# Graph attention with residual and layer norm on one core: own-column rows from the residual's x, a masked turn, and x loaded earlier

## The chip, the cores and the metric

The kernel runs on one core of one Trainium2 chip. Time is device time in microseconds of one execution, the median of several; the profiled execution has a time of its own and a span, which is the stretch from its first to its last recorded instruction.

## The reference

`x` is 4096 x 512, `adj` 4096 x 4096, W 512 x 2048, all float32. Four heads attend over all columns; `adj` is added to the scores.

```python
ht  = (h @ W).reshape(N, 4, 512).transpose(1, 0, 2)
e   = leaky_relu(src[:, :, None] + dst[:, None, :], 0.01) + adj_mat[None]
att = softmax(e, axis=-1)
h_prime = einsum('hij,hjd->hid', att, ht)          # then the mean over heads
x   = layernorm(x + h_prime.mean(0))
```

The entries of `adj` that aren't zero are uniform between 0.05 and 1e9. They are so far apart that the softmax of a row is 1 at the row's largest entry. So the kernel computes, for each row i with its largest column c: out[i] = layernorm(x[i] + x[c] @ (mean of the four heads' W)). It also tests that the largest entries lead by enough, and has a general path for when they don't; with these inputs that path isn't taken. Entries are more frequent at low columns, and the diagonal is always set: so some rows have a c below 128, and some have c = i.

## The kernel before

**Blocks.** The 4096 rows are 32 blocks of 128. Block 0 is rows 0 to 127; block ib from 1 on has on partition p the row 128 + 31 p + ib - 1. A loop over t from 0 to 31 (L546) does several stages for blocks at different distances: at t it reduces block t, looks up the column of block t - 2, and projects block t - 3.

**Loads.** One queue, SP's, takes adj (2 MiB a block, issued five blocks ahead, `load_adj`), W, x and at the end the output. `hold` keeps all of x in SBUF for the residual; W's rows lie in its blocks 16 to 31 at first. `x_at` (L532) says at which t four more blocks of x are queued, ahead of that t's adj: at t = 3, 7, 11, 15 and 18.

**Finding the column.** DVE reduces the 4096 entries of a row to maxima of segments (16 wide up to block 17, then 32, 64 in the last four; `segment_maxima`, L212), takes the largest and its place (L222, L224). POOL makes from the place a row number (`row`, L226) and gathers that segment (`lead`, L230) from `adj` again. Two blocks later DVE finds the place within the segment (L270), POOL adds both to the column (`col`, L272) and gathers the rows of x with these columns (`y`, L255 or L250). POOL runs in the order written, and so do all engines.

**The table.** In blocks 1 to 27 (`TABLED`) a row with c below 128 isn't gathered: `away` adds 8192 (`SKIP`) to its column, which the gather's bounds check drops. Its projected row comes from a table, x[0:128] @ W, held as three bf16 parts `z`: `low` is the place in the table, `spread` makes from it a 128 x 128 choice matrix `pick` (a matmul `px`, then two ACT operations `off` and `pick`), and three bf16 matmuls (L343) add the table's rows. So that the dropped rows of `y` are zero, ACT clears `y` beforehand (`clear_rows`, L245).

**Projection.** TensorE turns `y` by four transposes (`turned_rows`, L284, into `tp`), ACT copies the turn to `yt` (L286), TensorE adds the residual (L296), the table's rows (L343) and four 128 x 512 products with `w_sum` (L303), all into one PSUM tile. ACT takes the statistics and later writes the normalised rows (`finish`, L391).

**The end.** After the loop the last blocks are projected, some statistics go to DVE (`moments`, `factor`, `normalise`), and the last block is done in two halves (L400, L434, L440). `head_norms` gives the bound of the lead test, in three parts at t = 21, 22 and 23 (L473 to L489).

Of the kernel before, what the change touches and what calls it, by code (L numbers as in the profile page):

```python
# [9 lines left out]
F32 = mybir.dt.float32  # L10
BF16 = mybir.dt.bfloat16
U32 = mybir.dt.uint32
# [12 lines left out]
E_EARLY = 16  # L25
E_LAST = 64
EARLY = 18
LAST = 4
SKIP = 8192
TABLED = range(1, 28)  # L30


@with_exitstack
# [40 lines left out]
def leading_rows(ctx, tc, x, adj, W, a, out, ident, leads, any_bad):  # L74
# [23 lines left out]
    adj_pool = ctx.enter_context(tc.tile_pool(name="adj_pool", bufs=AHEAD + 1))  # L98
    y_pool = ctx.enter_context(tc.tile_pool(name="y_pool", bufs=6))
    lead_pool = ctx.enter_context(tc.tile_pool(name="lead_pool", bufs=1))  # L100
    LEADS = (8, 8, LAST)
    once = ctx.enter_context(tc.tile_pool(name="once", bufs=1))
    small = ctx.enter_context(tc.tile_pool(name="small", bufs=5))
    rows = ctx.enter_context(tc.tile_pool(name="rows", bufs=2))
# [44 lines left out]
    load_x(0, 1)  # L149
    for ib in range(KB // 2 + 1, AHEAD):  # L150
        load_adj(ib)
    load_x(1, Q - 1)

    make_identity(nc, ident)
    first = once.tile([P, NB], U32, name="first")
    for e, lo, hi in spans:
        if lo == 0:
            nc.gpsimd.iota(first[:, 0:1], pattern=[[0, 1]], base=0, channel_multiplier=N // e)
            lo = 1
        nc.gpsimd.iota(  # L160
            first[:, lo:hi], pattern=[[N // e, hi - lo]], base=(P + lo - 1) * N // e,
            channel_multiplier=RB * N // e,
        )
    ones = once.tile([P, P], F32, name="ones")
    nc.gpsimd.memset(ones, 1.0)
    width = once.tile([P, len(spans)], U32, name="width")
# [32 lines left out]
    low_of, pick_of = {}, {}  # L199

    def segment_maxima(ib, lo, hi):

# [14 lines left out]
    def find_segment(ib):  # L217
        if ib == NB - 1:
            nc.vector.max(out=top[:, ib, :], in_=best)
            return  # L220
        seg = seg_of.pop(ib)
        nc.vector.max(out=top[:, ib, :], in_=seg)  # L222
        at = at_of[ib] = small.tile([P, 8], U32, name="at")
        nc.vector.max_index(at, top[:, ib, :], seg)  # L224
        row = small.tile([P, 1], U32, name="row")
        nc.gpsimd.tensor_tensor(row, at[:, 0:1], first[:, ib : ib + 1], op=OP.add)  # L226
# [8 lines left out]
        start = at_of[ib] = small.tile([P, 1], U32, name="start")  # L235
        if ib in TABLED:
            away = small.tile([P, 1], F32, name="away")
            nc.gpsimd.tensor_scalar(away, at[:, 0:1], float(P // e), float(SKIP), op0=OP.is_lt, op1=OP.mult)
            nc.gpsimd.tensor_scalar(start, at[:, 0:1], float(e), away, op0=OP.mult, op1=OP.add)
        else:  # L240
            nc.gpsimd.tensor_tensor(start, at[:, 0:1], width[:, k : k + 1], op=OP.mult)

    def clear_rows(ib):
        y = y_t[ib] = y_pool.tile([P, D], F32, name="y")
        nc.scalar.copy(y, zero.to_broadcast([P, D]))  # L245

    def gather_rows(ib, col):
        if ib not in TABLED:
            y = y_t[ib] = y_pool.tile([P, D], F32, name="y")
            nc.gpsimd.indirect_dma_start(  # L250
                out=y, out_offset=None, in_=x,
                in_offset=bass.IndirectOffsetOnAxis(ap=col[:, :1], axis=0),
            )
            return
        nc.gpsimd.indirect_dma_start(  # L255
            out=y_t[ib], out_offset=None, in_=x,
            in_offset=bass.IndirectOffsetOnAxis(ap=col[:, :1], axis=0),
            bounds_check=N - 1, oob_is_err=False,
        )
        low = low_of[ib] = small.tile([P, 1], BF16, name="low")  # L260
        nc.gpsimd.tensor_scalar(low, col, float(SKIP - 1), float(SKIP - 1), op0=OP.max, op1=OP.subtract)

# [3 lines left out]
    def find_column(ib):  # L266
        if ib < BEHIND:
            find_inner(ib)
        within = small.tile([P, 8], U32, name="within")
        nc.vector.max_index(within, top[:, ib, :], lead_of[ib])  # L270
        col = small.tile([P, 1], U32, name="col")
        nc.gpsimd.tensor_tensor(col, at_of.pop(ib), within[:, 0:1], op=OP.add)  # L272
        gather_rows(ib, col)

    def find_column_in_row(ib):
# [2 lines left out]
        nc.vector.max_index(col, top[:, ib, :], adj_t[ib])  # L278
        gather_rows(ib, col)

    def turned_rows(y):
        tp = psum.tile([P, KB, P], F32, name="tp", bufs=2)
        for kb in range(KB):
            nc.tensor.transpose(tp[:, kb, :], y[:, ds(kb, P, KB)], ident)  # L284
        yt = rows.tile([P, KB, P], F32, name="yt")
        nc.scalar.copy(yt, tp)  # L286
        return yt

    def turn(ib):
        yt_of[ib] = turned_rows(y_t.pop(ib))  # L290

    def residual(ib):
        start = ib not in o_ps
# [35 lines left out]
    def spread(ib):  # L329
        where = psum.tile([P, P], F32, name="px", bufs=1)  # L330
        nc.tensor.matmul(where, low_of.pop(ib).to_broadcast([P, P]), ident_b, start=True, stop=True)  # L331
        off = rows.tile([P, P], F32, name="off")
        nc.scalar.activation(off, where, AF.Square, bias=minus)  # L333
        pick = pick_of[ib] = rows.tile([P, P], BF16, name="pick")
        nc.scalar.activation(pick, off, AF.Relu, bias=1.0, scale=-1.0)  # L335
# [193 lines left out]
    def report(pg):  # L529
        nc.vector.tensor_scalar(any_bad, pg, -1.0, float(N), op0=OP.mult, op1=OP.add)  # L530

    x_at = {lo - 1 - lo // (5 * Q): (lo, Q) for lo in range(Q, BEHIND, Q)}  # L532
    squares = list(range(KB * H))
    squares_at = {t: 2 if t < 7 else 1 for t in range(3, 15)}
    COLUMN, PROJECT, STATS = 2, 3, 4
# [10 lines left out]
    for t in range(NB):  # L546
        if t == NB // 2:
            tc.mark_branch_hint_location("general", engines=HINTED)
        if t in x_at:
            load_x(*x_at[t])  # L550
        if t + AHEAD == NB - 1:
            load_x(LATE, 2)
        load_adj(t + AHEAD)
        middle = PIECES if t in END else 1 if t == NB - 1 else 2
        segment_maxima(t, 0, middle)
        if t >= COLUMN and t not in END and t != COLUMN + 1:
            find_column(t - COLUMN)
# [12 lines left out]
        for lo, hi in FACTORS:  # L570
            if t == lag_of(hi):
                nc.vector.reciprocal(sd[:, lo:hi], sd[:, lo:hi])
                if hi < BEHIND:
                    scales(slice(lo, hi))
        if t < 2:
            mean_of_heads(t)
        elif t == 2:
            mean_of_heads(2)
            mean_of_heads(3)
            fill_table()  # L580
        if t == 0:
            square_sums_of_a()
        if 21 <= t < 24:
            head_norms(t - 21)
        ib = t - PROJECT
        if t == NB - 2:
            finish(BEHIND - 3)
            finish(BEHIND - 2)
        if t == NB - 1:
            row_norm(LATE)  # L590
            row_norm(LATE + 1)
            finish(BEHIND - 1)
            residual(LATE + 1)
        if ib >= 0:
            if ib in TABLED:
                spread(ib)
            turn(ib)
            if ib > BEHIND:
                products(ib - 1, KB - 1, KB)
            if ib < BEHIND:  # L600
                residual(ib)
            if ib in TABLED:
                from_table(ib)
            products(ib, 0, KB if ib < BEHIND else KB - 1)
            if ib == 0:
                split_table()
        for _ in range(squares_at.get(t, 0)):
            square_sum_of_w(squares.pop(0))
        if t >= BEHIND + STATS:
            put_by(t - STATS)  # L610
        elif t >= STATS:
            row_norm(t - STATS)
            parked_stats(t - STATS)
        for lo, hi in FACTORS:
            if t == hi - 1 + STATS:
                root(slice(lo, hi))
        for done in FINISHED.get(t, ()):
            finish(done)
# [253 lines left out]
```

## Time and profile before

| | us |
|---|---|
| median of 3 runs (233.75 to 234.14) | 233.87 |
| the profiled execution | 233.53 |
| its span | 232.0 |
| TensorE busy | 197.6 |
| DVE busy | 189.6 |
| ACT busy | 153.2 |
| POOL busy | 111.5 |
| moved by DMA: 96.04 MB, mean 414 GB/s | |

Engines are named PE (TensorE's matmuls), PEld (its weight loads), DVE, ACT, POOL and SP. In a timeline a row begins with its start and its duration in us; in brackets stands the engine's idle time just before it and what ended it. In the chain of waits a row begins with start and duration of one piece. In a list of groups a row gives the count, then busy us, the mean ns of one, and the idle time before them. A row of windows gives the stretch, its length, the busy time of PE, PEld, DVE, ACT and POOL with the counts, TensorE's granted clock, the DMA share and GB/s.

### The profile page before, as it was taken

The numbers are of one execution on the slowest core, as the hardware profiler recorded it, in microseconds if no ns is written. First come the engines' busy times: TensorE is split into PE (matmuls) and PEld (weight loads), VectorE is DVE, ScalarE is ACT, GpSimd is POOL, SyncE is SP. The second block draws the span as 40 slices with busy tenths as digits, with TensorE's granted clock in tenths as the row PEclk, the third lists the DMA queues.
The fourth block names the chain that finished last, engine by engine and source line by source line (L and its number), as shares of the span: only waits on it lengthen the run. The fifth ranks groups of instructions, "written<-read, shape, count | busy, mean of one in ns | idle before, by whom it ended". The sixth has DMA issues, their size and how long they took to land.

```text
span 232.0 us, 2532 instructions
## 1 busy us (share of the span) xinstructions
PE 197.6 (85%) x604; PEld 95.5 (41%) x614; DVE 189.6 (82%) x296; ACT 153.2 (66%) x378; POOL 111.5 (48%) x254
## 2 busy tenths in 40 slices
PE   0069988779099999997999899999999999999990
PEld 0033443334044444443444345454544444545460
DVE  0448289899879997999699959996999999967882
ACT  3003213588075987797998678878888877958872
POOL 4020414525554556355635665554565665637620
PEclk9999999999859999999999999999999999999997
DMA  6999999999999999999999999999999999999995
GB/s 221 426 435 428 433 421 437 425 431 411 440 429 422 420 437 427 429 421 434 418 433 430 417 435 429 419 430 431 426 432 415 419 425 416 419 416 419 420 374 207
DMA packets 13379, 96.04 MB, mean 414 GB/s; under 512 B 2148, under 2 KB 2596, under 8 KB 7984
## 3 DMA queue, kind: packets, MB, share of 16 engines
q1 hardware_dynamic: 9792, 88.08, 90.0%
q0 software_dynamic: 3552, 7.73, 8.5%
q8 instruction: 6, 0.10, 0.2%
q14 instruction: 13, 0.11, 0.1%
q10 hardware_dynamic: 16, 0.02, 0.0%
HBM read 88.51 MB, written 8.39 MB: 418 GB/s over the span
## 4 chain that ended last, share of the span: by engine, by line
DMA 44%; PE 30%; DVE 19%; ACT 2%; issue 1%; POOL 1%; DVEq 0%; POOLq 0%; ACTq 0%
DMA adj_t<-in_adj_dram 39%; PE o L303 19%; DVE seg L212 15%; DMA y<-in_x_dram,col 4%; PE o L296 3%; PE o L343 3%; PE tp L284 3%; PE o L400 2%; DVE at L224 1%; DVE top L222 1%; DMA a_rows<-in_L_gnn_a_dram 1%; DVE inner L264 1%; POOL lead L230 0%; PE o L396 0%; ACT sq L368 0%
## 5 line engine op out<-in xcount | busy, mean ns | idle before, releaser
L212 DVE TENSOR_REDUCE seg<-adj_t 128x128 f32<-128x2048 f32 (+4 forms) x54 | 138.9, 2589 | 27.4 <-DMA adj_t<-in_adj_dram 27.4
L303 PE MATMUL o<-w_sum,yt 128*128 128x512 f32 x248 | 113.5, 598 | 1.1 <-ACT yt L286 0.8
L303 PEld LDWEIGHTS o<-w_sum,yt 128*128 128x128 f32 x248 | 46.8, 192 | 49.0 <-issue 42.0
L230 POOL DMA_INDIRECT lead<-in_adj_dram,row x31 | 32.5, 1050 | 14.5 <-POOL row L226 14.5
L255 POOL DMA_INDIRECT y<-in_x_dram,col x27 | 29.1, 1077 | 12.1 <-POOL col L272 6.1
L226 POOL TENSOR_TENSOR row<-at,first 128x1 uint32<-128x1 uint32 x31 | 5.8, 188 | 60.0 <-DVE at L224 43.6
L284 PE MATMUL tp<-ident,y 128*128 128x128 f32 x128 | 22.9, 302 | 12.0 <-DMA y<-in_x_dram,col 11.9
L286 ACT COPY yt<-tp 128x512 f32<-128x512 f32 x33 | 19.0, 576 | 14.2 <-PE tp L284 13.9
L451 PE MATMUL o<-hold,ident 128*128 128x512 f32 x32 | 16.4, 671 | 14.0 <-DMA hold<-in_L_gnn_W_dram 14.0
L284 PEld LDWEIGHTS tp<-ident,y 128*128 128x128 f32 x128 | 18.3, 210 | 23.9 <-issue 17.8
L296 PE MATMUL o<-hold,ident 128*128 128x512 f32 x50 | 26.5, 612 | 0.0
L333 ACT ACTIVATE off<-px,minus 128x128 f32<-128x128 f32 x27 | 9.9, 366 | 19.9 <-PE px L331 19.8
L343 PE MATMUL o<-z,pick 128*128 128x512 bf16 x72 | 20.4, 386 | 1.1 <-ACT pick L335 0.8
L347 ACT ACTIVATE sq<-hold 128x512 f32<-128x512 f32 x32 | 20.0, 625 | 0.0
L391 ACT ACTIVATE hold<-hold,nm,sd 128x512 f32<-128x512 f32 x24 | 18.8, 801 | 0.0
L374 ACT ACTIVATE sq<-hold,nm 128x512 f32<-128x512 f32 x24 | 17.3, 722 | 0.8
L452 ACT ACTIVATE w_sum<-o 128x512 f32<-128x512 f32 x4 | 2.4, 597 | 22.5 <-PE o L451 22.5
L245 ACT COPY y<-zero 128x512 f32<-128x512 f32 x27 | 16.3, 603 | 0.0
L451 PEld LDWEIGHTS o<-hold,ident 128*128 128x128 f32 x32 | 6.7, 216 | 22.9 <-issue 21.6
L343 PEld LDWEIGHTS <-pick 128*128 128x128 bf16 x81 | 7.8, 100 | 19.9 <-issue 10.5
L372 ACT ACTIVATE hold<-o 128x512 f32<-128x512 f32 x24 | 14.3, 597 | 0.8
L222 DVE MAX8 top<-seg 128x8 f32<-128x256 f32 (+2 forms) x31 | 11.3, 366 | 1.1
(117 smaller groups left out, 190.3 us busy)
## 6 DMA issues: line engine op xcount, KB each, us to landing
adj_t<-in_adj_dram SPq DMA_DIRECT2D x28, 2048.0 KB, 33.1
adj_t<-in_adj_dram SPq DMA_DIRECT2D x6, 1024.0 KB, 27.3
out_dram<-hold SPq DMA_DIRECT2D x12, 512.0 KB, 10.1
hold<-in_x_dram SPq DMA_DIRECT2D x5, 1024.0 KB, 33.0
hold<-in_L_gnn_W_dram SPq DMA_DIRECT2D x2, 2048.0 KB, 16.5
hold<-in_x_dram SPq DMA_DIRECT2D x4, 512.0 KB, 12.7
adj_t<-in_adj_dram SPq DMA_DIRECT2D x4, 512.0 KB, 18.6
out_dram<-hold SPq DMA_DIRECT2D x4, 256.0 KB, 2.8
```

The source lines that it names most:

```text
L212: nc.vector.tensor_reduce(seg_of[ib][:, ts(k, N // e // n)], adj_t[ib][:, ts(k, N // n)].rearrange("p (s e) -> p s e", e=e), axis=AX.X, op ...
L230: nc.gpsimd.indirect_dma_start(out=lead, out_offset=None, in_=adj_segs[e], in_offset=bass.IndirectOffsetOnAxis(ap=row[:, :1], axis=0),)
L255: nc.gpsimd.indirect_dma_start(out=y_t[ib], out_offset=None, in_=x, in_offset=bass.IndirectOffsetOnAxis(ap=col[:, :1], axis=0), bounds_che ...
L284: nc.tensor.transpose(tp[:, kb, :], y[:, ds(kb, P, KB)], ident)
L286: nc.scalar.copy(yt, tp)
L296: nc.tensor.matmul(o_ps[ib], ident, hold[:, ib, :], start=start, stop=False)
L303: nc.tensor.matmul(o_ps[ib], yt_of[ib][:, kb, :], w_sum[:, kb, :], start=(start and kb == 0), stop=(kb == KB - 1),)
L343: nc.tensor.matmul(o_ps[ib], pick, z[k], start=(start and k == 0), stop=False)
L347: nc.scalar.activation(sq, hold[:, ib, :], AF.Square, accum_out=xx[:, ib : ib + 1])
L374: nc.scalar.activation(sq, hold[:, ib, :], AF.Square, bias=nm[:, i], scale=-float(D), accum_out=sd[:, i])
L391: nc.scalar.activation(hold[:, ib, :], o, AF.Identity, bias=nm[:, i], scale=sd[:, i])
L451: nc.tensor.matmul(o, ident, hold[:, w_at + kb * H + h, :], start=(h == 0), stop=(h == H - 1))
```

## The change

- `OWNED` is blocks 4 to 17. There a row whose column is its own row number isn't gathered: POOL compares the column with `own`, a constant, and adds 8192 where they agree (`skipped`, `asked`). Its row of x is in `y` beforehand, since ACT copies the residual's x to `y` in place of zero.
- So `y` holds x also in the rows that come from the table. The turn leaves these out: POOL makes `kept`, a diagonal matrix with 1 where the row's column is below 8192, and TensorE multiplies by it in ordinary f32 matmuls in place of the transposes.
- x must be there sooner: the first load takes blocks 1 to 7, blocks 8, 12 and 16 follow at t = 2, 6 and 10, and block 20 stays at t = 18.
- Blocks 18 and 19 are no longer in the table: all their rows are gathered, and `clear_rows`, `low`, `spread` and the three table matmuls fall away.
- Segments are 64 wide from block 24 on (before from 28).
- `head_norms` runs at t = 16, 17 and 18. `off` is bf16 with one buffer, and there are fewer buffers for `lead`. At the end two finishes stand ahead of a block's moments.

```diff
@@
-LAST = 4
+LAST = 8
 SKIP = 8192
-TABLED = range(1, 28)
+TABLED = (*range(1, 18), *range(20, 28))
+OWNED = range(4, 18)
...
-    LEADS = (8, 8, LAST)
+    LEADS = (4, 4, LAST - 1)
...
-    load_x(1, Q - 1)
+    load_x(1, 2 * Q - 1)
...
+    own = once.tile([P, len(OWNED)], F32, name="own")
+    nc.gpsimd.iota(
+        own, pattern=[[1, len(OWNED)]], base=P + OWNED[0] - 1, channel_multiplier=RB,
+        allow_small_or_imprecise_dtypes=True,
+    )
...
     def clear_rows(ib):
         y = y_t[ib] = y_pool.tile([P, D], F32, name="y")
-        nc.scalar.copy(y, zero.to_broadcast([P, D]))
+        nc.scalar.copy(y, hold[:, ib, :] if ib in OWNED else zero.to_broadcast([P, D]))
+
+    def leave_out_own(ib, col):
+        skipped = small.tile([P, 1], F32, name="skipped", bufs=2)
+        k = ib - OWNED[0]
+        nc.gpsimd.tensor_scalar(skipped, col, own[:, k : k + 1], float(SKIP), op0=OP.is_equal, op1=OP.mult)
+        asked = small.tile([P, 1], U32, name="asked", bufs=2)
+        nc.gpsimd.tensor_scalar(asked, col, skipped, None, op0=OP.add)
+        return asked
+
+    def keep_gathered(ib, col):
+        kept = kept_of[ib] = rows.tile([P, P], F32, name="kept")
+        nc.gpsimd.tensor_scalar(kept, ident, float(SKIP), col, op0=OP.mult, op1=OP.is_gt)
...
+        asked = leave_out_own(ib, col) if ib in OWNED else col
         nc.gpsimd.indirect_dma_start(
             out=y_t[ib], out_offset=None, in_=x,
-            in_offset=bass.IndirectOffsetOnAxis(ap=col[:, :1], axis=0),
+            in_offset=bass.IndirectOffsetOnAxis(ap=asked[:, :1], axis=0),
             bounds_check=N - 1, oob_is_err=False,
         )
+        if ib in OWNED:
+            keep_gathered(ib, col)
...
-            nc.tensor.transpose(tp[:, kb, :], y[:, ds(kb, P, KB)], ident)
+            if kept is None:
+                nc.tensor.transpose(tp[:, kb, :], y[:, ds(kb, P, KB)], ident)
+            else:
+                nc.tensor.matmul(tp[:, kb, :], y[:, ds(kb, P, KB)], kept, start=True, stop=True)
...
-        off = rows.tile([P, P], F32, name="off")
+        off = rows.tile([P, P], BF16, name="off", bufs=1)
...
-    x_at = {lo - 1 - lo // (5 * Q): (lo, Q) for lo in range(Q, BEHIND, Q)}
+    x_at = {2: (8, 4), 6: (12, 4), 10: (16, 4), 18: (20, 4)}
...
-        if 21 <= t < 24:
-            head_norms(t - 21)
+        if 16 <= t < 19:
+            head_norms(t - 16)
...
+    finish(BEHIND + 2)
+    finish(LATE - 1)
     moments(NB - 2)
-    finish(BEHIND + 2)
     stats_of_half(NB - 1, 0)
     factor(NB - 2)
     normalise(NB - 2, o_ps.pop(NB - 2))
-    finish(LATE - 1)
```

On SP the x loads (128x2048) move ahead. Before, from the load of x's blocks 8 to 11 to that of blocks 16 to 19, with block 12's adj the first and block 19's the last between them (the numbers after adj_t only tell tiles apart):

```order
L135 DMA hold_68<-in_x_dram 128x2048
L128 DMA adj_t_492<-in_adj_dram 128x4096
L128 DMA adj_t_550<-in_adj_dram 128x4096
L128 DMA adj_t_607<-in_adj_dram 128x4096
L128 DMA adj_t_664<-in_adj_dram 128x4096
L135 DMA hold_68<-in_x_dram 128x2048
L128 DMA adj_t_725<-in_adj_dram 128x4096
L128 DMA adj_t_784<-in_adj_dram 128x4096
L128 DMA adj_t_841<-in_adj_dram 128x4096
L128 DMA adj_t_898<-in_adj_dram 128x4096
L135 DMA hold_68<-in_x_dram 128x2048
```

Now, from block 14's adj to the load of x's blocks 20 to 23, which stands before block 23's adj as it did:

```order
L129 DMA adj_t_627<-in_adj_dram 128x4096
L136 DMA hold_68<-in_x_dram 128x2048
L129 DMA adj_t_691<-in_adj_dram 128x4096
L129 DMA adj_t_757<-in_adj_dram 128x4096
L129 DMA adj_t_822<-in_adj_dram 128x4096
L129 DMA adj_t_885<-in_adj_dram 128x4096
L129 DMA adj_t_948<-in_adj_dram 128x4096
L129 DMA adj_t_1014<-in_adj_dram 128x4096
L129 DMA adj_t_1080<-in_adj_dram 128x4096
L129 DMA adj_t_1146<-in_adj_dram 128x4096
L136 DMA hold_68<-in_x_dram 128x2048
```

The load of x's blocks 16 to 19 stood ahead of block 20's adj and stands ahead of block 15's now; eight blocks of adj follow it without x between them.

On POOL, one pass of the loop in the middle, from the row number of block t to the place in the table of block t - 2, before:

```order
L226 TENSOR_TENSOR row<-at,first 128x1
L230 DMA lead_617<-in_adj_dram,row 128x16
L238 TENSOR_SCALAR away<-at 128x1
L239 TENSOR_SCALAR start<-at,away 128x1
L272 TENSOR_TENSOR col<-start,within 128x1
L255 DMA y<-in_x_dram,col 128x512
L261 TENSOR_SCALAR low<-col 128x1
```

and now:

```order
L232 TENSOR_TENSOR row<-at,first 128x1
L236 DMA lead_701<-in_adj_dram,row 128x16
L245 TENSOR_SCALAR away<-at 128x1
L246 TENSOR_SCALAR start_f<-at,away 128x1
L297 TENSOR_SCALAR col_f<-within,start_f 128x1
L258 TENSOR_SCALAR skipped<-col_f,own 128x1
L260 TENSOR_SCALAR asked<-col_f,skipped 128x1
L276 DMA y<-in_x_dram,asked 128x512
L265 TENSOR_SCALAR kept<-ident,col_f 128x128
L284 TENSOR_SCALAR low<-col_f 128x1
```

Two operations stand between the column and its gather, and one between the gather and `low`.

On TensorE, the end of block 17 and blocks 18 and 19, now:

```order
L315 MATMUL tp<-kept,y 128x128 x4
L327 MATMUL o<-hold,ident 128x512
L374 LDWEIGHTS pick
L374 MATMUL o<-z_151,pick 128x512
L374 LDWEIGHTS pick
L374 MATMUL o<-z_152,pick 128x512
L374 LDWEIGHTS pick
L374 MATMUL o<-z_153,pick 128x512
L334 MATMUL o<-w_sum,yt 128x512 x4
L313 MATMUL tp<-ident,y 128x128 x4
L327 MATMUL o<-hold,ident 128x512
L334 MATMUL o<-w_sum,yt 128x512 x4
```

Block 17 is turned by `kept`; blocks 18 and 19 are turned by transposes and have no table rows, so that the last three rows stand twice (one of them is shown). Before, each of these blocks had the rows of block 17, with transposes by `ident` in place of `kept`.

More of the change, by code (lines that the diff above doesn't have):

```diff
@@ L198, in leading_rows @@
     seg_of, at_of, lead_of, y_t, yt_of, o_ps = {}, {}, {}, {}, {}, {}
-    low_of, pick_of = {}, {}
+    low_of, pick_of, kept_of = {}, {}, {}
     def segment_maxima(ib, lo, hi):
@@ L234, in find_segment @@
         lead_of[ib] = lead
-        start = at_of[ib] = small.tile([P, 1], U32, name="start")
+        owned = ib in OWNED
+        start = at_of[ib] = small.tile([P, 1], F32 if owned else U32, name="start_f" if owned else "start")
         if ib in TABLED:
@@ L270, in find_column @@
         nc.vector.max_index(within, top[:, ib, :], lead_of[ib])
-        col = small.tile([P, 1], U32, name="col")
-        nc.gpsimd.tensor_tensor(col, at_of.pop(ib), within[:, 0:1], op=OP.add)
+        start = at_of.pop(ib)
+        if ib in OWNED:
+            col = small.tile([P, 1], F32, name="col_f", bufs=2)
+            nc.gpsimd.tensor_scalar(col, within[:, 0:1], start, None, op0=OP.add)
+        else:
+            col = small.tile([P, 1], U32, name="col")
+            nc.gpsimd.tensor_tensor(col, start, within[:, 0:1], op=OP.add)
         gather_rows(ib, col)
@@ L279, in find_column_in_row, with turned_rows @@
         gather_rows(ib, col)
-    def turned_rows(y):
+    def turned_rows(y, kept=None):
         tp = psum.tile([P, KB, P], F32, name="tp", bufs=2)
         for kb in range(KB):
-            nc.tensor.transpose(tp[:, kb, :], y[:, ds(kb, P, KB)], ident)
+            if kept is None:
+                nc.tensor.transpose(tp[:, kb, :], y[:, ds(kb, P, KB)], ident)
+            else:
+                nc.tensor.matmul(tp[:, kb, :], y[:, ds(kb, P, KB)], kept, start=True, stop=True)
         yt = rows.tile([P, KB, P], F32, name="yt")
@@ L289, in turn @@
     def turn(ib):
-        yt_of[ib] = turned_rows(y_t.pop(ib))
+        yt_of[ib] = turned_rows(y_t.pop(ib), kept_of.pop(ib, None))
     def residual(ib):
```

## The prediction

> **What bounds the kernel now.** I read the page's head and slices first, then the chain of waits from its end, then the windows and waits of the stretch that the chain names.
>
> ```profile
> span 232.0 us, 2532 instructions
> DMA  6999999999999999999999999999999999999995
> ```
>
> The DMA engines are busy in every slice but the first and the last, so a first reading says: bytes bound it. The chain says something else about the last third:
>
> ```profile
> 139.45 9.32 DMA y<-in_x_dram,col
> ...
> 148.91 0.72 PE tp L284 x4
> ...
> 150.49 0.65 PE o L343 x3
> 151.13 3.43 PE o L303 x8
> 154.57 0.13 PE o L475 x2
> 154.70 0.31 PE o L476 x2
> ...
> 155.17 0.53 PE tp L284 x4
> ...
> 160.65 0.06 PE px L331
> 160.70 0.54 PE tp L284 x4
> ...
> 166.24 0.54 PE tp L284 x4
> ...
> 222.91 3.73 PE o L400 x16
> ```
>
> The turn (tp) at 148.91 is block 17's, released by that block's gather; 155.17, 160.70 and 166.24 are blocks 18, 19 and 20. From there the chain is TensorE, 5.53 us a block. Its idle time in the window from 149 to 221 us:
>
> ```profile
> 149.00:221.00 72.00, 71.35 (x234) 35.37 (x238) 64.08 (x116) 57.43 (x143) 41.22 (x85) 1.00 1.02 423
> PE tp L284 <- DMA y<-in_x_dram,col: 0.4, 1, 0.4
> ```
>
> TensorE is busy 71.35 of 72 us at clock 1.00 (first PE column), and so is the DMA (share 1.02, 423 GB/s). Its one wait for a gather in there is block 17's. So whatever makes that turn start later, and is not taken out of TensorE's work behind it, ends the program later. Before block 17, from block 4's turn at 71.7 on, TensorE still waits for gathers:
>
> ```profile
> PE tp L284 <- DMA y<-in_x_dram,col: 3.7, 6, 1.3
> ```
>
> **x sooner.** DVE's reductions show when a block of adj is there (blocks 12, 15, 16, 17, 18, 19, 20 and 23, in this order):
>
> ```profile
> 90.17 4.42 DVE L212 TENSOR_REDUCE seg<-adj_t 128x256 f32<-128x4096 f32 x1 [1.42 <-DMA adj_t<-in_adj_dram]
> 107.06 4.39 DVE L212 TENSOR_REDUCE seg<-adj_t 128x256 f32<-128x4096 f32 x1
> 114.50 4.42 DVE L212 TENSOR_REDUCE seg<-adj_t 128x256 f32<-128x4096 f32 x1 [1.77 <-DMA adj_t<-in_adj_dram]
> 120.12 4.42 DVE L212 TENSOR_REDUCE seg<-adj_t 128x256 f32<-128x4096 f32 x1
> 125.74 4.40 DVE L212 TENSOR_REDUCE seg<-adj_t 128x128 f32<-128x4096 f32 x1
> 131.15 4.40 DVE L212 TENSOR_REDUCE seg<-adj_t 128x128 f32<-128x4096 f32 x1
> 139.07 2.29 DVE L212 TENSOR_REDUCE seg<-adj_t 128x64 f32<-128x2048 f32 x1 [2.51 <-DMA adj_t<-in_adj_dram]
> 158.53 2.29 DVE L212 TENSOR_REDUCE seg<-adj_t 128x64 f32<-128x2048 f32 x1 [2.00 <-DMA adj_t<-in_adj_dram]
> ```
>
> Four blocks of x are 1 MiB, at 423 GB/s 2.48 us of the one queue. Before, the waits at 16, 20 and 23 are these loads. In the changed order adj of blocks 16 to 19 stands behind one x load more than before, and adj 15 behind two; from 20 on the count is as it was. Between 90.17 and 114.50 lie four adj blocks and one x load: (24.33 - 2.48) / 4 = 5.46 us a block, so adj 15 landed near 106.6. Two loads more make 111.5; less the rows that are not gathered any more by then (105 of the 145 below, 0.5 us) 111.0. DVE then needs its own pace, 5.62 us a block with segments of 16 and 5.41 with 32, and the head norms' operations, which move from blocks 21 to 23 to blocks 16 to 18; of five groups the first and the last:
>
> ```profile
> L473 DVE TENSOR_SCALAR each<-ident,aa 8x8 f32<-8x8 f32 x1 | 0.2, 199 | 0.0
> L489 DVE TENSOR_REDUCE vn<-both 128x1 f32<-128x4 f32 x1 | 0.2, 157 | 0.0
> ```
>
> 0.85 us in all. Block 19 starts at 111.0 + 5.62 x 3 + 5.41 + 0.85 = 134.1 in place of 131.15: **+2.95 us**. Block 23, with no extra load ahead, keeps its landing or gains the saved bytes.
>
> **POOL.** One pass of POOL, block 19's, with the gather of block 17 in it, and the one row for a 128x128 operation:
>
> ```profile
> 136.43 0.19 POOL L226 TENSOR_TENSOR row<-at,first 128x1 uint32<-128x1 uint32 x1 [0.40 <-DVE inner L264]
> ...
> 138.25 0.25 POOL L238 TENSOR_SCALAR away<-at 128x1 f32<-128x1 uint32 x1
> 138.60 0.27 POOL L239 TENSOR_SCALAR start<-at,away 128x1 uint32<-128x1 uint32 x1
> ...
> 139.45 1.08 POOL L255 DMA_INDIRECT y<-in_x_dram,col  x1 [0.44 <-POOL col L272]
> 140.61 0.23 POOL L261 TENSOR_SCALAR low<-col 128x1 bf16<-128x1 uint32 x1
> 3.01 0.57 POOL L182 TENSOR_SCALAR minus_b<-ident 128x128 bf16<-128x128 f32 x1
> ```
>
> `skipped` and `asked` come ahead of the gather, at 0.35 us from start to start each (138.25 to 138.60): +0.7. `kept` stands behind it, +0.67 by L182's row with the gap; it waits for the turn two blocks back, and `low`, the next `row` and the next gather are queued behind it. A pass grows from 4.4 to 5.8 us, more than DVE's 5.62, so POOL also falls behind, by 0.2 a pass plus the 0.6 of the scales; blocks 18 and 19, out of the table, give back 0.35 each. Between nothing and 1 us of backlog I take 0.5. The gather of block 13 belongs to block 15's pass: 111.0 + 5.3 to that pass's `row` as in block 19 (136.43 less 131.15) + 0.3 for segments of 16, then 3.0 (136.43 to 139.45) + 0.7 to the gather: 120.3. Landing takes:
>
> ```profile
> DMA to landing us min/median/max: 6.1/8.4/9.3
> ```
>
> so 128.7. The gather of block 17: 139.45 + 2.95 + 0.7 + 0.5 - 0.35 = 143.25, landed 151.7.
>
> **The masked turn.** Four transposes take 0.53 us, 0.134 each. An ordinary f32 matmul is two instructions here: 512 columns 0.43 each (L303, 3.43 / 8), 256 columns 0.233 (L400, 3.73 / 16), 16 columns 0.065 (L475). For 128 columns that gives 0.107 (a quarter of L303) up to the transposes' own 0.134: eight of them 0.86 to 1.07. The added cost is 0.33 to 0.54 a block, I take 0.45, nearest to two instructions in place of one at this size. Nothing is the lower bound, should the pair overlap wholly; two instructions in place of one of the same kind can't be a gain. Blocks 4 to 17 gain 14 x 0.45 = 6.3 us of TensorE work against the 3.7 of waits: even with every gather in time TensorE would be late.
>
> The Trainium skill ("TensorE: Matmul & The Clock Gate", Terms) has transpose mode as four times faster for FP32. By that the masked turn would be 2.13 us, +1.6 a block; the trace's 512-column rows put the factor at 1.6 to 2, and I go by them.
>
> **Sum.** TensorE from block 13's turn: 128.7 + 4 x 5.98 = 152.6 for block 17, a little after its gather, in place of 148.91. Block 18: + 5.98 = 158.6 (155.17 before, with the 0.44 of L475 and L476, which move ahead). Blocks 18 and 19 lose L343 and px, 0.71 each: 163.4 and 168.2 for blocks 19 and 20, against 160.70 and 166.24. So TensorE is 2.0 us late at block 20, with a slack of 0.26 at the last block's gather:
>
> ```profile
> 221.28 0.72 PE L284 MATMUL tp<-ident,y 128*128 128x128 f32 x4 [0.26 <-DMA y<-in_x_dram,col]
> ```
>
> That leaves **+1.7 us**.
>
> Edits at nothing: the copy of x in place of zero is the same 128x512 on ACT; its first one, block 4's, waits for the x load behind adj 4, and the turn's copy of block 0 waits behind it on ACT. What hides that is TensorE's longest wait, ahead of block 3's turn:
>
> ```profile
> 63.42 1.10 PE L284 MATMUL tp<-ident,y 128*128 128x128 f32 x4 [5.76 <-DMA y<-in_x_dram,col]
> ```
>
> Without that cover it would cost up to the 2.5 us of the load. The saved gathers: counting the reference's inputs, 145 rows of blocks 4 to 17 have their own column as maximum, and 47 rows of blocks 18 and 19 are now fetched that came from the table; 98 rows net.
>
> ```profile
> q0 software_dynamic: 3552, 7.73, 8.5%
> ```
>
> 8.5% of 16 x 232 engine-us over 3552 packets is 89 ns; 98 x 89 / 16 = 0.5 us of DMA, which ends no wait of TensorE. Segments of 64:
>
> ```profile
> L222 DVE MAX8 top<-seg 128x8 f32<-128x128 f32 x10 | 3.0, 295 | 0.3
> L224 DVE FIND_INDEX8 at<-top,seg 128x8 uint32<-128x128 f32 x10 | 2.8, 285 | 0.0
> L222 DVE MAX8 top<-seg 128x8 f32<-128x64 f32 x3 | 0.7, 228 | 0.1
> L224 DVE FIND_INDEX8 at<-top,seg 128x8 uint32<-128x64 f32 x3 | 0.7, 220 | 0.0
> ```
>
> 0.13 us a block, 0.5 over four, on a DVE whose gathers then land ahead of a TensorE that is late. The finishes that move ahead of a square root let a pair of blocks be stored sooner; the last store is block 31's, behind L400 at 222.91, and keeps its place.
>
> The profiled execution took 233.53 us, 0.34 under the median 233.87. 233.53 + 1.7 = 235.2 for such an execution, **235.6** as a median.
>
> **Rivals.**
> *Faster: the bytes show.* If gathers land sooner by more than their rows, or the turn is as cheap as the transposes and POOL's additions hide, TensorE reaches block 20 early and the end moves with DVE and DMA: 0.5 of bytes, 0.25 of head norms out of block 23, up to 0.5 from the segments; adj's landing holds it to some 0.6. It decides once block 17's turn starts before 150.6 us (+ 5.98 + 2 x 4.82 = 166.2). For it: the DMA row of nines. Against: 2.95 us of delay stands ahead of that gather. 233.2.
> *No change.* A masked turn of 0.53 and no POOL backlog or addition: gather at 142.4, turn 150.8, block 20 at 150.8 + 5.53 + 2 x 4.82 = 166.0. It is the lower bound of both prices at once. 233.8.
> *POOL waits for TensorE.* `kept` has two buffers. Once a turn starts more than about 3.6 us after its gather landed (two blocks of 5.98 less 8.4 of landing), POOL stands, and the next `row`, gather and so DVE and the adj queue behind it, and every later block repeats it: 235.6 + 3 for three blocks of 1 us, 238.6. By my sum TensorE is 0.9 behind at block 17; it needs a turn of 0.53 + 0.45 + (3.6 - 0.9) / 4 = 1.65 us.
> *Long masked turns.* If an instruction of 128 columns were held as long as one of 256 (0.233, L400), the turn would take 8 x 0.233 = 1.86, +1.33 a block: 14 x 1.33 = 18.6, less 3.7 of waits and 1.4 of the table, 247. L475's 0.065 for 16 columns speaks against so high a floor. The Trainium skill's four times, on the same page, would make some 251.
>
> **How the numbers follow.** Forecast 0.57; faster 0.18; no change 0.14; POOL waits 0.08; long masked turns 0.03. The forecast's own range comes from 0.33 with a landing 0.5 us under the median to 0.54 with one of 9.3: 234.5 to 237.0. To leave no more than 2 in 10 out it reaches from 233.2 (most of the faster case) to 237.8. A measurement of this kernel tells 0.2% (0.47 us) from no change: faster 0.18, same 0.14, slower 0.57 + 0.08 + 0.03 = 0.68.
>
> **What would show it.** In the changed profile: DVE's reduction of block 19 near 134 us, that of block 23 near 158; the gather of block 17 issued at 143 and its turn near 152.6; tp groups of 0.86 to 1.07 us in blocks 4 to 17; TensorE again without waits from there to the last block. Wrong would make it: a turn of block 17 before 150.6 us, waits of TensorE for gathers behind block 20 (then DVE or DMA bounds the end), or tp groups at 0.53.

## The result: 249.5 us, and the profile after

The changed kernel takes 249.52 us (median of 4 runs, 248.75 to 249.75) beside 234.0 us for the kernel before. The ratio is 1.0659 with a 95% interval of 1.0633 to 1.0685: 15.5 us slower, where 1.7 us was forecast. The direction was right, the size was not; the time lies beside the rival that had been given a chance of 0.03.

The page of the changed kernel, first the head and the slices of TensorE and DMA, then the group of the masked turns (`kept`), and from the list of groups that of the plain ones (`ident`):

```profile
span 248.1 us, 2669 instructions
...
PE   0079980689899999999999999999999999999990
...
DMA  6999999999999999999999999999999999955053
...
L315 PE MATMUL tp<-kept,y 128*128 128x128 f32 x112 | 29.2, 404 | 1.3 <-DMA y<-in_x_dram,asked 1.3
```

```profile
L313 PE MATMUL tp<-ident,y 128*128 128x128 f32 x72 | 12.4, 294 | 0.9 <-DMA y<-in_x_dram,col 0.9
```

The DMA engines now run dry before the end (5, 5, 0, 5, 3 in the last five slices), where before they were busy to the last one; TensorE stays busy up to the last slice. The fourteen masked turns (112 instructions) cover 29.2 us, 2.09 each with the overlap into what follows; a plain one (72 instructions, 18 turns, 12.4 us) covers 0.69 by the same count.

The chain of waits of the same kernel (start, length, what) shows what a block now costs on TensorE. Blocks 9, 10, 17, 18, 19 and 20:

```profile
109.05 1.92 PE tp L315 x8
110.97 0.86 PE o L327 x2
111.83 0.65 PE o L374 x3
112.48 3.43 PE o L334 x8
115.91 0.06 PE px L362
115.97 1.92 PE tp L315 x8
...
164.90 1.92 PE tp L315 x8
...
171.76 0.47 PE tp L313 x4
...
176.60 0.47 PE tp L313 x4
...
181.51 0.53 PE tp L313 x4
```

A block lasts 115.97 - 109.05 = 6.92 us in place of 5.53, and the whole difference is the turn: 1.92 in place of 0.53, 0.24 us for each of the eight instructions. Block 17's turn starts at 164.90 (148.91 before, 152.6 forecast), block 20's at 181.51 (166.24 before): + 15.3, and that is carried to the end. The stretches that these rows come from:

```profile
100.00:149.00 49.00, 49.00 (x159) 29.11 (x158) 37.35 (x58) 34.78 (x89) 34.49 (x75) 1.00 1.01 427
149.00:200.00 51.00, 51.00 (x164) 26.86 (x163) 45.20 (x69) 38.36 (x94) 31.43 (x72) 1.00 1.01 423
```

TensorE (the first column behind the length) is busy without a gap from 100 us on, at clock 1.00: the masked turns have made it the bound 50 us sooner than in the kernel before.

The weight loads suggest where the 0.24 us of an instruction of 128 columns come from. First those of the changed kernel's masked turn, then those of a plain turn in the kernel before:

```profile
108.83 1.94 PEld L315 LDWEIGHTS tp<-kept,y 128*128 128x128 f32 x8 [0.33 <-issue]
```

```profile
148.88 0.56 PEld L284 LDWEIGHTS tp<-ident,y 128*128 128x128 f32 x4 [0.92 <-PE px L331]
```

Eight loads back to back fill 1.94 us, 0.24 each, with no idle time between them: the matmuls and their loads go in step. Four loads for the transposes fill 0.56. Which of the two sets the pace, and what makes it so long, none of the forecast's rows showed, and the experiments had to find it.

### The profile page after: what moved, and what is told of

The parts are those of the page before. It is cut to its first block, busy times and chain, and to the rows that moved or that the text cites. A ratio compares the mean times of both kernels' runs of the same rounds, so it can differ in the third digit from the quotient of the medians.

```text
span 248.1 us, 2669 instructions
## 1 busy us (share of the span) xinstructions
PE 213.9 (86%) x662; PEld 113.7 (46%) x662; DVE 189.5 (76%) x296; ACT 151.6 (61%) x372; POOL 131.3 (53%) x293
## 2 busy tenths in 40 slices
DMA packets 13235, 95.90 MB, mean 387 GB/s; under 512 B 2155, under 2 KB 2539, under 8 KB 7840
## 4 chain that ended last, share of the span: by engine, by line
PE 61%; DMA 20%; issue 6%; POOL 4%; DVE 4%; ACT 2%; SPq 0%; POOLq 0%
PE o L334 34%; DMA adj_t<-in_adj_dram 13%; PE tp L315 9%; PE o L327 7%; PE o L374 6%; DMA y<-in_x_dram,col 4%; DMA y<-in_x_dram,asked 3%; PE tp L313 3%; DVE seg L218 2%; POOL lead L236 2%; PE o L431 2%; POOL y L276 1%; PE px L362 1%; POOL away L245 0%; DVE inner L287 0%
## 5 line engine op out<-in xcount | busy, mean ns | idle before, releaser
L315 PE MATMUL tp<-kept,y 128*128 128x128 f32 x112 | 29.2, 404 | 1.3 <-DMA y<-in_x_dram,asked 1.3
L315 PEld LDWEIGHTS tp<-kept,y 128*128 128x128 f32 x112 | 27.2, 326 | 6.1 <-issue 3.3
L482 PE MATMUL o<-hold,ident 128*128 128x512 f32 x32 | 16.3, 669 | 14.3 <-DMA hold<-in_L_gnn_W_dram 14.3
L327 PE MATMUL o<-hold,ident 128*128 128x512 f32 x50 | 25.6, 593 | 0.0
L364 ACT ACTIVATE off<-px,minus 128x128 bf16<-128x128 f32 x25 | 9.1, 366 | 16.9 <-PE px L362 16.8
L276 POOL DMA_INDIRECT y<-in_x_dram,asked x14 | 15.2, 1088 | 6.9 <-POOL asked L260 5.4
L374 PEld LDWEIGHTS <-pick 128*128 128x128 bf16 x75 | 7.2, 98 | 18.9 <-issue 11.1
L276 POOL DMA_INDIRECT y<-in_x_dram,col x11 | 11.9, 1081 | 6.3 <-POOL col L300 3.3
L313 PEld LDWEIGHTS tp<-ident,y 128*128 128x128 f32 x72 | 10.5, 208 | 6.9 <-issue 5.1
(128 smaller groups left out, 249.5 us busy)
```

What stands on the lines that cost most here:

```text
L276: nc.gpsimd.indirect_dma_start(out=y_t[ib], out_offset=None, in_=x, in_offset=bass.IndirectOffsetOnAxis(ap=asked[:, :1], axis=0), bounds_c ...
L315: nc.tensor.matmul(tp[:, kb, :], y[:, ds(kb, P, KB)], kept, start=True, stop=True)
L327: nc.tensor.matmul(o_ps[ib], ident, hold[:, ib, :], start=start, stop=False)
L374: nc.tensor.matmul(o_ps[ib], pick, z[k], start=(start and k == 0), stop=False)
L482: nc.tensor.matmul(o, ident, hold[:, w_at + kb * H + h, :], start=(h == 0), stop=(h == H - 1))
```

## The experiments

Theory A, formed on these rows: the masked turn is the mis-sized term and explains all of the 13.8 us between forecast and result. Theory B: the additions on POOL, or x sooner, cost several us as well, and the long turns hide them. All ratios are against the kernel before, run beside them on the same chip (medians 234.04 to 234.06).

### The turn alone, and everything but the turn

**Ordinary matmuls in the kernel before.** The edit, for blocks 4 to 17 alone:

```
-            nc.tensor.transpose(tp[:, kb, :], y[:, ds(kb, P, KB)], ident)
+            nc.tensor.matmul(tp[:, kb, :], y[:, ds(kb, P, KB)], ident, start=True, stop=True)
```

> The kernel before, with only the turn of blocks 4 to 17 changed from four transposes to four ordinary f32 matmuls with the identity; nothing on POOL, no other edit; the same numbers are computed. Theory A: + 14 x 1.39 = 19.5 us of TensorE, less the 4.1 us that it waited for gathers from block 4 to 17: + 15.4, about 249.2. Rival B (part of the 15.5 us comes from POOL, x or the table): 238 to 246. The prediction's own price (+0.45 a block): 236.

Measured: 247.75 us, ratio 1.0593 (1.0577 to 1.0609), + 13.7. Turns of 1.92 us from block 4's at 71.74 to block 17's at 161.61: 89.87 / 13 = 6.91 a block, so 5.53 + 1.39 as in the changed kernel. TensorE's own waits in that stretch took up 5.3 us (71.72 to 148.91 is 77.2 for 13 blocks of 5.53), a little more than the 4.1 expected. The exchange of transposes for ordinary matmuls, with nothing else changed, is worth nearly all of the result. Theory A holds this far.

**The changed kernel with transposes**, POOL's masks still made:

```
-                nc.tensor.matmul(tp[:, kb, :], y[:, ds(kb, P, KB)], kept, start=True, stop=True)
+                nc.tensor.transpose(tp[:, kb, :], y[:, ds(kb, P, KB)], ident)
```

> The changed kernel with the turn of blocks 4 to 17 back to four transposes; POOL still makes the masks, x is still sooner, 18 and 19 still out of the table. The mask is left out, so rows of these blocks that the table serves get their own row of x added. Theory A (the masked turn alone is the mis-sized term: 1.92 us in the changed trace in place of 0.53): tp groups of 0.53, the rest as the prediction's sum without its masked term: block 17's turn about 151.7, block 20 near 166.9, time 233.8 to 234.8. Rival B (the additions on POOL or the earlier x cost several us as well, hidden behind the long turns): 236 or more, with waits of TensorE for gathers behind block 17.

Measured: 241.34 us, ratio 1.0303 (1.0282 to 1.0323), + 7.3. Theory A expected at most 234.8. So a second cost of some 7 us stood behind the first, and theory B has a part in it. POOL's timeline in that run, from block 16's `row` to block 17's, with the gather of block 14 between them (start, length, idle time before and what ended it):

```profile
126.88 0.19 POOL L232 TENSOR_TENSOR row<-at,first 128x1 uint32<-128x1 uint32 x1
127.35 1.07 POOL L236 DMA_INDIRECT lead<-in_adj_dram,row  x1 [0.28 <-POOL row L232]
128.50 0.24 POOL L245 TENSOR_SCALAR away<-at 128x1 f32<-128x1 uint32 x1
128.85 0.27 POOL L246 TENSOR_SCALAR start_f<-at,away 128x1 f32<-128x1 uint32 x1
129.23 0.29 POOL L297 TENSOR_SCALAR col_f<-within,start_f 128x1 f32<-128x1 uint32 x1
129.62 0.31 POOL L258 TENSOR_SCALAR skipped<-col_f,own 128x1 f32<-128x1 f32 x1
130.02 0.29 POOL L260 TENSOR_SCALAR asked<-col_f,skipped 128x1 uint32<-128x1 f32 x1
130.83 1.08 POOL L276 DMA_INDIRECT y<-in_x_dram,asked  x1 [0.51 <-POOL asked L260]
131.97 0.75 POOL L265 TENSOR_SCALAR kept<-ident,col_f 128x128 f32<-128x128 f32 x1
132.81 0.23 POOL L284 TENSOR_SCALAR low<-col_f 128x1 bf16<-128x1 f32 x1
133.13 0.19 POOL L232 TENSOR_TENSOR row<-at,first 128x1 uint32<-128x1 uint32 x1
```

From `row` to `row` are 6.25 us, and nothing in it waits for another engine: the gaps of 0.28 and 0.51 are POOL's own, ahead of a gather. POOL's gathers go at this pace from block 6's at 79.71 to block 12's at 117.82 (38.11 / 6 = 6.35, with the two small operations for the scales that follow some passes), and block 17's is issued at 148.89, where 143.25 was forecast and 139.45 stood before. From 75.75 to 145.51 no `row` waits for DVE any more, so nothing takes the lateness up in between. The busy time would not have told it: 61.3 us of the 83 between 66 and 149, some three quarters.

**The same without `kept` on POOL** (with transposes nothing reads it):

```
-        if ib in OWNED:
-            keep_gathered(ib, col)
```

> The run with the turn by transposes, and without the 128x128 mask on POOL (which nothing reads there). The mask is left out, so rows that the table serves get their own row of x added. Theory P (in that run POOL is what bounds blocks 5 to 17: a pass of 6.25 us without a wait, row to row, so each pass adds to the lateness): pass 6.25 - 0.84 = 5.41, under DVE's 5.62, POOL waits for DVE again, the gather of block 17 goes from 148.9 to 143 to 145, time 241.3 to 234.5 to 236. Theory H (DVE is held: the head norms, moved to blocks 16 to 18, make DVE wait for their products on TensorE, which stand behind a late turn, 4.6 us in that run): the gather of block 17 stays past 146, time 237.5 or more. Theory X (x sooner is what costs): time stays at 239 or more.

Measured: 236.55 us, ratio 1.0099 (1.0064 to 1.0135), + 2.5. One operation off POOL gives 4.8 us back; block 17's gather is issued at 143.66, as theory P had it. POOL's pass is the second cost, shown by the removal of its longest addition. Theory H (DVE waits for the head norms' products on TensorE) is not what held this run: that wait shrinks from 4.6 to 0.9 us by itself. So part of the 4.8 may have come by way of it, set off by POOL's late gathers; how much was not separated. The time is a little above P's range, too.

**x sooner alone**, in the kernel before:

```
-    load_x(1, Q - 1)
+    load_x(1, 2 * Q - 1)
...
-    x_at = {lo - 1 - lo // (5 * Q): (lo, Q) for lo in range(Q, BEHIND, Q)}
+    x_at = {2: (8, 4), 6: (12, 4), 10: (16, 4), 18: (20, 4)}
```

> The kernel before with only the loads of x in the changed order: seven blocks ahead of block 5's adj, then 8, 12 and 16 ahead of adj 7, 11 and 15. The prediction's step: DVE's reduction of block 19 at 131.15 + 2.95 - 0.85 (no head norms) = 133.3, block 23 unchanged; gather of block 17 at 141.6, its turn about 150.0, block 20 near 167.4, + 1.1: 235.0. Rival: the delay is taken up by waits that are there anyway: 233.5 to 234.4. Theory X (x sooner alone costs several us): 236 or more.

Measured: 235.88 us, ratio 1.0076 (1.006 to 1.0093), + 1.8. DVE's reduction of block 15 starts at 111.42 (adj 15 was forecast there at 111.0 to 111.5), of block 19 at 133.69 (133.3 expected), of block 23 at 158.59 (158.53 before). Its chain:

```profile
150.66 0.72 PE tp L284 x4
156.92 0.53 PE tp L284 x4
162.45 0.53 PE tp L284 x4
167.98 0.53 PE tp L284 x4
```

Block 17's turn at 150.66 (150.0 expected), block 20's at 167.98 (167.4), 1.74 behind the 166.24 of before. The landings were read rightly; the price at the end is 0.7 us above the expected one, and it is as much alone as the whole forecast.

### What makes the masked turn's loads long

Three theories stood for the 0.24 us of an instruction with 128 columns: its weight load (W), the columns streamed (C, and L for load and stream one after the other), and the step of four elements with which the load goes through y (S). In the kernels with 64 columns four transposes fill the tile first, and half of it stays unmasked. In those without a step, or with a step of two, products go with other rows of W than they should.

```
 as changed      nc.tensor.matmul(tp[:, kb, :], y[:, ds(kb, P, KB)], kept, ...)
 64 columns      nc.tensor.matmul(tp[:, kb, : P // 2], y[:, ds(kb, P, KB)], kept[:, : P // 2], ...)
 no step         nc.tensor.matmul(tp[:, kb, :], y[:, ts(kb, P)], kept, ...)
 step of two     nc.tensor.matmul(tp[:, kb, :], y[:, ds(kb // 2 * 2 * P + kb % 2, P, 2)], kept, ...)
 no step, 64     nc.tensor.matmul(tp[:, kb, : P // 2], y[:, ts(kb, P)], kept[:, : P // 2], ...)
```

> The changed kernel; ahead of the eight instructions of each masked turn stand four transposes that fill the tile, and the eight stream 64 columns of the mask in place of 128 (the other half of the tile is left unmasked). Theory W (each instruction lasts as long as the load of its own 128 columns of weights, 0.24 us, however few columns are streamed): tp groups 0.47 + 1.92 = 2.4 us, time 249.5 + 11 x 0.47 = 254 to 256. Theory C (time goes with the columns streamed, 0.24 for 128, so 0.12 for 64): 0.47 + 0.96 = 1.43, time about 243 to 245. Theory L (load and stream one after the other, 0.13 + 0.107): 0.47 + 1.49 = 1.96, time about 250.

> The changed kernel, with the turn of blocks 4 to 17 taking its weights from 128 neighbouring columns of y in place of every fourth one (so these blocks' products go with other rows of W than they should). Theory W: no change, tp groups 1.92, time 249.5. Theory S (the step of four elements makes the load of weights slow; loads of neighbouring columns are shown with 0.19): groups of 1.55 or less, time 245.5 or less.

> The changed kernel with the masked turn's weights taken from every second column of y (so products go with other rows of W). Runs so far: a step of four 0.24 us an instruction, neighbouring columns 0.119. Theory B (the load's time goes with the bytes that it passes over, four times as many with a step of four): 0.12 to 0.13, tp groups 0.95 to 1.05, time about 240. Theory A (any step makes the load slow): 0.24, groups 1.92, time 249.5.

> The changed kernel with the masked turn's weights from neighbouring columns and only 64 columns of the mask streamed, behind four transposes that fill the tile (as in the run with 64 columns and the step of four, where the eight instructions took 1.80 us). Theory 1 (neighbouring columns: the 128 streamed columns set the 0.119): the eight take 0.43 to 0.55, tp groups with the transposes about 1.0. Theory 2 (the load itself takes about 0.11 also without a step): the eight take 0.85 to 0.95, groups 1.35 to 1.45.

One row of each run's chain, in this order: the eight masked instructions in steady work.

```profile
97.76 1.80 PE tp L318 x8
```

```profile
150.32 0.95 PE tp L315 x8
```

```profile
152.13 1.00 PE tp L315 x8
```

```profile
115.26 0.84 PE tp L318 x8
```

| step | columns streamed | eight instructions | each |
|---|---|---|---|
| 4 | 128 | 1.92 us | 0.24 us |
| 4 | 64 | 1.80 us | 0.225 us |
| 2 | 128 | 1.00 us | 0.125 us |
| 1 | 128 | 0.95 us | 0.119 us |
| 1 | 64 | 0.84 us | 0.105 us |

Half the columns save 0.015 us an instruction: C and L fall. The step of four doubles it, a step of two hardly costs anything, so W holds in the form of S: the instruction goes at the pace of its weight load, some 0.105 us for 128 neighbouring f32 columns, and 0.225 to 0.24 with 16 bytes from one column to the next. (The 0.105 is no floor of every instruction: L475's two in the forecast's rows, the first of which had been loaded under a longer instruction, took 0.065 each.) Theory S had expected 1.55, from a 0.19 that is the length of a single load, not its pace; theory B of the step of two is right in the figure, but by its reason (the bytes passed over) a load of neighbours would take 0.06, and the last run shows 0.105, as its theory 2 had it (0.84 for the eight, 0.85 to 0.95 expected).

This price of the step is shown for ordinary f32 matmuls alone. The transposes load the same columns with the same step, and their four loads fill 0.56 us, 0.14 each. Why the step of four doubles the one and not the other, no run here settles.

The Trainium skill ("TensorE: Matmul & The Clock Gate", LDWEIGHTS) gives a load as its columns divided by 1.2 in ns. For 128 that is an estimate of 107 ns, and the 0.105 of the last run agrees. The formula counts columns and nothing else; at a step of four the measured 0.24 decides.

The times: 257.18, 240.05, 242.23 and 244.58 us, one run each. With the step gone the turn is 0.95 and the kernel is still 6.0 us slower than before: TensorE then waits for gathers again (4.3 us in seven waits), and POOL issues these some 6.2 us apart, as in the run with transposes. In the run with 64 columns and step four, `kept` waited 9.1 us for TensorE, the forecast's third rival; in the changed kernel itself it was 1.7 us in two waits.

### Three mends, and the small edits alone

**The changed kernel, whole, with three mends:** weights from neighbouring columns with W loaded to match, `kept` made on DVE behind the next block's reduction, and the head norms at blocks 21 to 23 again. The turn's edit is the line "no step" above; two more:

```
-    w_blocks = W.rearrange("(p kb) (h d) -> p (kb h) d", p=P, h=H)
+    w_blocks = W.rearrange("(kb p) (h d) -> p kb h d", p=P, h=H)
...
-        nc.gpsimd.tensor_scalar(kept, ident, float(SKIP), col, op0=OP.mult, op1=OP.is_gt)
+        nc.vector.tensor_scalar(kept, ident, float(SKIP), col, op0=OP.mult, op1=OP.is_gt)
```

> The changed kernel with its whole result kept, and three things mended: the turn's weights from neighbouring columns (W loaded to match), the 128x128 mask made on DVE behind the next block's reduction, the head norms at blocks 21 to 23 as before. If the step of the weights and POOL's pass are the two causes: masked groups of 0.95, POOL pass 5.4, block 17's turn at 152 to 153, as the prediction's sum: 234.5 to 236. If the saved bytes then show: 233.3 to 233.8. If something else costs several us: 237 or more.

Measured: 238.45 us, ratio 1.0183 (1.0166 to 1.02), + 4.4: 11.1 of the 15.5 us are gone, and the rest stays. This run has close to the prices that the forecast had assumed (the turn 0.95, a POOL pass without a wait 5.57 beside 5.8), and so checks its sum:

```profile
147.73 0.95 PE tp L317 x8
153.68 0.95 PE tp L317 x8
160.01 0.59 PE tp L315 x4
164.97 0.44 PE tp L315 x4
169.84 0.44 PE tp L315 x4
```

A block of 5.95 (5.98 forecast), block 17's gather at 142.44 (143.25) and turn at 153.68 (152.6), block 20 at 169.84 (168.2; the head norms' 0.44 lies behind block 17 again). At block 20 it is 3.6 us late in place of 2.0. The further 0.8 us to the median were not traced to a cause.

**The small edits, in the kernel before.** Turns without the step (W loaded to match); the table without blocks 18 and 19; and all that the change does except own rows, x sooner and head norms (table, segments of 64 from block 24 with fewer buffers, finishes ahead of the last square root). The main lines of the second and third:

```
-TABLED = range(1, 28)
+TABLED = (*range(1, 18), *range(20, 28))
...
-LAST = 4
+LAST = 8
...
-    LEADS = (8, 8, LAST)
+    LEADS = (4, 4, LAST - 1)
```

> The kernel before, with every turn taking 128 neighbouring columns of y in place of every fourth one, and W loaded in the order that goes with it (the same result). If the step of four slows the transposes' loads as it does the ordinary matmuls': tp groups of 0.43 to 0.47 in place of 0.53; the last gather, with its slack of 0.26, lets through no more than 0.3 us: 233.6 to 234.1. If the step does nothing to transposes: groups of 0.53, 234.0. If the loads of W in pieces half as long cost at the start: 234.5 to 236.

> The kernel before with only blocks 18 and 19 out of the table. The prediction's term: TensorE loses 2 x 0.71 = 1.4 us behind block 17's turn, but the last block's gather, which it waited 0.26 us for, lets no more than 0.3 of that through; 47 more gathered rows are 47 x 89 / 16 ns = 0.26 us of DMA: 233.8 to 234.3 beside 234.06. Rival (the end hangs on TensorE's work more than that slack says): 232.6 to 233.2.

> The kernel before with blocks 18 and 19 out of the table, segments of 64 columns from block 24 (with the fewer buffers that go with them) and the finishes ahead of the last square root; x in its old order, no own rows, no masks, head norms where they were. The prediction's terms: TensorE 1.4 us ahead, DVE 0.5 us ahead over blocks 24 to 27, adj's landing lets some 0.3 to 0.6 through: 233.3 to 233.9. Rival (the last gather and the DMA's bytes bound the end): 233.9 to 234.5. Rival (fewer buffers for the gathered segments hold POOL or DVE): 234.6 or more.

Measured: 234.56 (1.0012, 0.9991 to 1.0034), 234.05 (0.9997, 0.9988 to 1.0006) and 234.76 us (1.0034, 1.0021 to 1.0048). The first makes a plain turn 0.44 us where it was 0.53, so transposes pay for the step too, a sixth of their time; nothing of it reaches the end. The second takes 1.4 us off TensorE, and TensorE then waits for gathers 14.6 us in place of 11.9:

```profile
PE tp L284 <- DMA y<-in_x_dram,col: 14.6, 15, 6.5
```

(This execution took 235.33 us, 1.3 above the median.) That the end lets nothing through is as forecast, but the slack at the last gather is not its only reason. In the third run the last turn starts at 220.94 (221.28 before) and waits for no gather. ACT's copy of it then stands behind a finish and starts at 222.41 (222.29 before), and TensorE waits 0.48 us for it:

```profile
223.02 3.72 PE L400 MATMUL o<-w_sum,yt 128*128 128x256 f32 x16 [0.48 <-ACT yt L286]
```

So nothing is won there (222.91 before). The third is 0.7 us slower, a miss. In its profiled run the last stores land later (3.8 us beside 2.6 for the two of 256 KB), but so they do with the table alone (3.6), whose median is unchanged. Which of its edits costs the 0.7 us stays open. None of the three is better than the kernel before.

## Why the forecast was right in direction and wrong in size

- **What bounds the kernel.** Right. From block 17 on TensorE's lateness went through to the end: + 15.3 us at block 20, + 15.5 in the median. And TensorE's own savings gain nothing (the table alone).
- **The masked turn: this step failed.** The forecast took 0.45 us more a block; it is 1.39. It priced the eight instructions by the columns streamed, from rows L303, L400 and L475, which all load neighbouring columns, and put the weight load, as a term of its own, at nothing without a reason. The turn loads every fourth column. Without the step the price is 0.95, inside the 0.86 to 1.07 of the forecast, but that is luck: with half the columns the eight still take 0.84, so there, too, the load and not the streaming sets the pace. The row that was used as the strongest argument against a floor, L475's 0.065 for 16 columns, was no steady pace: its two loads are

```profile
153.98 0.19 PEld L475 LDWEIGHTS o<-ww,ones 128*128 128x128 f32 x1 [0.24 <-issue]
154.41 0.19 PEld L475 LDWEIGHTS o<-ww,ones 128*128 128x128 f32 x1 [0.24 <-issue]
```

  so the first had been hidden under an instruction of 512 columns. The row below it in the forecast's own chain, L476, spoke the other way: two instructions of 8 columns took 0.31 us, 0.155 each, far more than 8 columns by the streaming price.
- **The rival with long masked turns.** It came out (247 forecast, 249.5 measured) with the right size, 1.86 beside 1.92, by luck: it held an instruction of 128 columns as long as one of 256, while the length comes from the load. Its chance of 0.03 rested on L475. The Trainium skill's factor of four ("TensorE: Matmul & The Clock Gate", Terms) had given an estimate of 2.13 and some 251 us, which the forecast set aside for the streaming price; measured are 1.92 / 0.53 = 3.6 with the step, and 0.95 / 0.44 = 2.2 without it on both sides.
- **POOL: mis-sized, and hidden in the result.** The pass is 6.25 us in place of 5.8: `skipped`, `asked` and the gap ahead of the gather add 0.97 (col_f to gather 1.60 in the rows above, col to gather 0.63 before; 0.7 taken), and `kept` with its gap 0.84 (0.67 taken). The worse error was to add the backlog once, as 0.5, counted from block 15 on: a pass that is longer than the blocks' pace adds its difference in each block, and here it did so from block 8's pass on. With the turn back at 0.53 all the other edits together made + 7.3, where less than 1 us was expected.
- **x sooner.** The landings of adj were right, each within 0.5 us; the turns came 0.6 to 0.7 us later than expected, and the end + 1.8 in place of + 1.1.
- **Head norms.** Priced as 0.85 us of DVE. Not foreseen: their products on TensorE now stand behind a late turn, and DVE waits for them, with the next reduction queued behind:

```profile
DVE w L511 <- PE o L507: 9.6, 1, 9.6
```

  So block 19's reduction starts at 143.14 in the changed kernel, in place of the forecast's 134.1. TensorE was the bound by then, and what this costs alone was not measured.
- **Edits at nothing.** The table: right. The finishes and segments: not shown to be free (+ 0.7 together). The copy of x: its wait for the load was longer than priced (ACT stood 7.79 us, and TensorE 8.73 behind it), but the cover held: block 4's turn starts at 73.22, and at 73.53 with x sooner alone, where there is no such copy. The saved bytes: 95.90 MB in place of 96.04, at 423 GB/s an estimated 0.3 us, too little to show beside the rest.

The costs don't add up, because each bound hides the next: + 13.7 for the turn alone, + 7.3 for all the rest, + 15.5 together.

## What to carry to other kernels

A short matmul is to be priced by its weight load as well as by its columns, and from a row whose stationary operand is read in the same layout; a row in which the load hides under a long neighbour is no price. An engine's work that repeats in every block is compared with the blocks' pace start to start, gaps included, and the difference is multiplied by the number of blocks. And where a term has one price far above the others, the run without that term is worth making first: here it uncovered a second bound of half the size.

## What the runs showed of the hardware

- In a row of short ordinary f32 matmuls, each with its load of 128 weight columns: 0.105 us for neighbours, 0.125 or less with every second column, 0.225 to 0.24 with every fourth (16 bytes apart). The jump between a step of two and of four was not expected.
- Transposes feel the step less: 0.134 us each with a step of four, 0.11 with neighbours. The reason is open.
- A 128x128 f32 operation with a column of scalars took 0.75 us on POOL, and 0.28 on DVE.
